# A sparse two-layer graph kernel: gather groups of 8 rows by 64 places, and the first head's relu on ScalarE

## The chip, the core and the metric

The kernel runs on one NeuronCore of a Trainium2 chip. Five engines work side by side, each on its own in-order list of instructions: TensorE (PE; its weight loads are shown as PEld), VectorE (DVE), ScalarE (ACT), GpSimd (POOL) and SyncE (SP). [...] The metric is device time in microseconds of one whole execution, as the median of several runs. A profiled execution gives a trace with every instruction; its span begins with the first and ends with the last of them.

## What is computed

Two graph layers over 3327 nodes with 128 features. The adjacency matrix is dense in memory but has only some 64 non-zero entries in a row. The first layer is an attention layer with four heads, and it holds nearly all of the work. Cut to what matters:

```python
h = jnp.maximum(_layernorm(x, axis=-1), 0.0)
def _gatv2_head(x, A_shape, w1, w2, a, Wlin):          # x is h here
    x1 = x @ w1
    x2 = x @ w2
    E = jax.nn.leaky_relu(x1[:, None, :] + x2[None, :, :], negative_slope=0.01)
    s = E @ a
    s = jnp.tanh(s / 8.0) * 8.0
    s = jnp.exp(s) * A_shape
    s = s / jnp.sum(s, axis=-1, keepdims=True)
    out = s @ x @ Wlin.T
    return jax.nn.leaky_relu(out, negative_slope=0.01)
x = x + jnp.concatenate([head(...) for 4 heads], axis=-1) @ w
# layer 1: relu(A_norm @ (h @ W.T + b)), A_norm from (adj + I) by row sums; x = x + that
```

Only pairs with a non-zero adjacency count, so the kernel makes scores for those pairs alone. With `leaky(e) = slope*e + (1-slope)*relu(e)`, a score is a linear part, which is made once for each node, and `(1-slope) * a . relu(x1 + x2)`, which has to be made for each pair and head.

## The kernel before

**Blocks, places and windows.** The 3328 padded rows are 26 blocks (`NB`) of 128 rows, and a block is done in two halves (`hb`) of 64 rows. While one block is scored, the next is prepared (`prep`, from line 353): its adjacency block is transposed in pieces on TensorE (line 365), copied by ScalarE (line 367) and stored by a DMA that ScalarE issues (line 370); VectorE finds the non-zero columns of each row with MAX8 and MATCH_REPLACE8 (lines 422 to 456). The result is a list `idx` with 64 places for each row; rows with more neighbours have the rest done in an overflow group.

**Gathers.** A table in HBM has one row for each node: its features, its four projections `x2` (one for each head), a linear score part, and columns of adjacency. A window `w` (four for a half block, `NW`) is a tile `g` of 8 slices; slice `t` is one indirect DMA (line 597) issued by GpSimd that brings 128 table rows onto the 128 partitions: 8 graph rows by 16 places. In the kernel before, the 8 slices of a window are the 64 rows of the half, and the four windows are the places 0 to 15, 16 to 31 and so on. Four buffers of `g` exist; a buffer is given back (`allow("g")`) behind the window's aggregation at line 702.

**Groups.** A half block is 9 groups: `m` = 0 to 7 are halves of windows (4 slices, so 512 pairs), `m` = 8 is the overflow. So there are 26 x 2 x 9 = 468 groups, and 26 x 2 x 8 = 416 of them are of the ordinary kind. `stage_z` does this for a pair of heads `hp` at a time:

- a PSUM tile `z` of two banks, one for each head of the pair (`ps_z`, two buffers);
- for each of the two heads four transposes on TensorE (line 624), which turn the projections of 4 slices, pairs on partitions, into features on partitions and 512 pairs along the row;
- one VectorE operation over both heads (line 640), `r = max(z, -x1)`, with `x1n = -x1` broadcast along the 16 places. As `max(z, -x1) = relu(z + x1) - x1`, the missing `x1` is a linear term, and `pex` (lines 563 to 570) adds it in the form `a . x1`.

`stage_r` (line 645) multiplies `r` by the vector `a` of each head (line 653, into the score tile `s`), one group later than `stage_z`. `finish` (line 657), once for each window, copies the scores to SBUF on ScalarE (line 662), transposes them back (line 671), adds the linear parts on VectorE (lines 674, 677), does tanh and exp on ScalarE (lines 682, 684), makes weights on VectorE (line 693) and aggregates the window on TensorE (line 702): eight matmuls, slice `t` into the column group `t % 4` (32 rows of PSUM each).

**What sets the order.** The order in each engine's list is written out by hand (`manual_schedule`). `slot()` (line 858) is called at six places of each group and gives out one step each of what is in progress: the `finish` of earlier windows, the tail of a half block (`close`), the preparation of the next block (`advance`), and the gathers. One `slot()` stands between the first and the second head's transposes of each pair (line 632). The framework puts in the semaphore waits, from which tile an instruction writes and which it reads.

**The queues.** GpSimd issues all gathers, 68 for a block. SyncE and ScalarE issue the other DMAs; a DMA that ScalarE issues stands in the same list as its arithmetic.

Of the kernel before, what the change touches and what calls it, by code (L numbers as in the profile page):

```python
# [9 lines left out]
F32 = mybir.dt.float32  # L10
AF = mybir.ActivationFunctionType
OP = mybir.AluOpType
# [3 lines left out]
P = 128  # L16
# [45 lines left out]
HALF = 64  # L62
OVT = 3
FOUND = 2
FEAT = 64
BODY = 648
# [165 lines left out]
def _sparse_layers(tc, nc, x, adj, w1, w2, a, wlin, w, gw, gb, gb_sb, gwT, x_sb, dinv, flag, ident, out):  # L232
# [24 lines left out]
    with ExitStack() as l0:  # L257
# [95 lines left out]
        def prep(b, k):  # L353
# [204 lines left out]
            for h in range(H):  # L558
                nc.tensor.matmul(pm[:, h * P:(h + 1) * P], w1_sb[:, h, :], hTb, start=True, stop=True)
            x1n = pb.tile([P, H, P], F32, name="x1n")  # L560
            nc.scalar.activation(x1n, pm[:, :H * P].rearrange("p (h i) -> p h i", h=H), AF.Copy, scale=-1.0)
            pmx = pb.tile([P, 16, H], F32, name="pmx")
            nc.vector.tensor_tensor(pmx, tmask[:, :, None].to_broadcast([P, 16, H]),
                                    p_all[:, b, None, :H].to_broadcast([P, 16, H]), OP.mult)
            yield
            yield
            pm = bank()
            nc.tensor.matmul(pm[:, :16 * H], modsel, pmx.rearrange("p t h -> p (t h)"), start=True, stop=True)
            pex = pb.tile([P, 16, H], F32, name="pex")
            nc.scalar.copy(pex, pm[:, :16 * H].rearrange("p (t h) -> p t h", h=H))  # L570
            k.x1b, k.x1n, k.pex = x1b, x1n, pex
            yield

        def rows_in():
            state["turn"] += 1
            return pgs[state["turn"] % 4].tile([P, WT, WIDE], F32, name="g")

        def gather(b, hb, w):

            k = blks[b]  # L580
            tab = tables[b % 2].rearrange("(r u) -> r u", u=1)
            if w == NW:
                if b + hb == 0:
                    state["over"] = pe_.tile([P, OVT, WIDE], F32, name="ge")
                    nc.vector.memset(state["over"][HALF:, FOUND:], 0.0)
                g, n, at = state["over"], FOUND, k.idxo[:, hb]
                rows = b * P + HALF * hb
                c0, n0 = (0, FEAT + COLS) if hb == 0 else (FEAT, BODY + FEAT)
                nc.sync.dma_start(g[:HALF, FOUND, :n0], tables[b % 2][:NP * ROW].rearrange("(r c) -> r c", c=ROW)[rows:rows + HALF, c0:c0 + n0])
            else:  # L590
                g, n, at = rows_in(), WT, k.idx[:, w, WT * hb:WT * hb + WT]

            def one(t):
                lo, hi = (0, FEAT + COLS) if hb == 0 else (0, BODY + FEAT)
                if w < NW:
                    lo, hi = (8 * t, hi) if hb == 0 else (0, BODY + 8 * t + 8)
                return nc.gpsimd.indirect_dma_start(out=g[:, t, lo:hi], out_offset=None, in_=tab,  # L597
                                                    in_offset=bass.IndirectOffsetOnAxis(ap=at[:, t:t + 1], axis=0))

            queue.extend((k, hb, w, partial(one, t)) for t in range(n))  # L600
            k.g[hb, w] = g
# [10 lines left out]
        def stage_z(k, hb, m, slot):  # L612
            n = 4 * P if m < 8 else FOUND * P
            arrived(k, hb, m // 2)
            g = k.g[hb, m // 2]
            out = []
            for hp in range(2):
                z = ps_z.tile([P, 2, BANK], F32, name="z")
                r = pr.tile([P, 2, BANK], F32, name=f"r{hp}")
                for i in range(2):  # L620
                    h = 2 * hp + i
                    c0 = k.f0[hb] + PROJ + h * D
                    for q in range(n // P):
                        nc.tensor.matmul(z[:, i, q * P:(q + 1) * P], g[:, m % 2 * 4 + q, c0:c0 + D], ident,  # L624
                                         is_transpose=True, start=(q == 0 or m < 8), stop=(m < 8), skip_group_check=True)
                    if m == 8:
                        nc.tensor.matmul(z[:, i, n:n + HALF], g[:HALF, FOUND, c0:c0 + D], ident[:HALF, :HALF],
                                         is_transpose=True, start=False, stop=False, skip_group_check=True)
                        nc.tensor.matmul(z[:, i, :n], k.x1b[:, h * D:(h + 1) * D], k.oi[:, hb * n:(hb + 1) * n],  # L629
                                         start=False, stop=True, skip_group_check=True)  # L630
                    if i == 0:
                        slot()
                slot()
                if m == 8:
                    nc.vector.tensor_tensor(r[:, :, n:n + HALF], z[:, :, n:n + HALF],  # L635
                                            k.x1n[:, 2 * hp:2 * hp + 2, HALF * hb:HALF * hb + HALF], OP.max)
                    nc.scalar.activation(r[:, :, :n], z[:, :, :n], AF.Relu)  # L637
                else:
                    r0 = HALF * hb + 32 * (m % 2)
                    nc.vector.tensor_tensor(r.rearrange("p h (i s) -> p h i s", s=16), z.rearrange("p h (i s) -> p h i s", s=16),  # L640
                                            k.x1n[:, 2 * hp:2 * hp + 2, r0:r0 + 32, None].to_broadcast([P, 2, 32, 16]), OP.max)
                out.append(r)
            return out

# [12 lines left out]
        def finish(k, hb, w):  # L657
# [1 line left out]
            f0 = k.f0[hb]  # L659
            nt, nk, nm = (WT, 4, 2) if w < NW else (OVT, OVT, 1)  # L660
            ssb = ph.tile([P, BANK], F32, name="ssb", bufs=1)
            nc.scalar.copy(ssb[:, :nk * P], s[:, :nk * P])  # L662
            if w < NW:
                wq = pb.tile([P, WT, 8], F32, name="wq")
                diag = bass.AP(g.tensor, g.offset + BODY * hb, [list(g.ap[0]), [WIDE + 8, 8], [1, 8]])
                nc.vector.tensor_tensor(wq, diag, qmask[:, None, :].to_broadcast([P, WT, 8]), OP.mult)
            yield
            yield
            pt = ps_tr.tile([P, 4, P], F32, name="tr")
            for q in range(nk):  # L670
# [3 lines left out]
            nc.vector.tensor_tensor(sc[:, :nt].rearrange("p (m k) h -> p m k h", m=nm),  # L674
                                    pt.rearrange("p k (h m) -> p m k h", m=32)[:, :nm, :nk],
                                    g[:, :, f0 + D:f0 + D + H].rearrange("p (m k) h -> p m k h", m=nm), OP.add)
            nc.vector.tensor_add(sc[:, :nt], sc[:, :nt], k.pex[:, 8 * hb:8 * hb + 8] if w < NW else  # L677
                                 k.ex[:, OVT * hb:OVT * hb + OVT, 42:42 + H])
            yield
            yield  # L680
            th = pb.tile([P, WT, H], F32, name="th")
# [9 lines left out]
            if w < NW:  # L691
                wt = pv.tile([P, WT, H, 8], F32, name="wt", bufs=2)
                nc.vector.tensor_tensor(wt, pe[:, :, :, None].to_broadcast([P, WT, H, 8]),  # L693
                                        wq[:, :, None, :].to_broadcast([P, WT, H, 8]), OP.mult)
                yield
                yield
                yield
                yield
                yield
                for t in range(WT):  # L700
                    u, cg = t // 4, t % 4
                    nc.tensor.matmul(ag[32 * cg:32 * cg + 32, u, :WORK], wt[:, t].rearrange("p h q -> p (h q)"),  # L702
                                     g[:, t, f0:f0 + WORK], start=(w == 0 and t < 4), stop=False, skip_group_check=True)
                allow("g")
                return
            am = pb.tile([P, OVT, HALF], F32, name="am", bufs=1)
# [649 lines left out]
```

## Time and profile before

| what | value |
|---|---|
| three runs: median, lowest, highest | 2523.51, 2521.55, 2527.58 us |
| the profiled execution: time, and its span | 2520.29 us, 2518.6 us |
| mean granted TensorE clock | 0.982 |
| VectorE busy, 400 to 2000 us, in stretches of 400 us | 352.23, 350.61, 351.86, 355.88 us |
| ScalarE busy, same stretches | 118.22, 110.82, 118.83, 111.55 us |
| DMA share, same stretches | 0.97, 0.97, 0.97, 0.98 |
| gathers, line 597: count, mean | 1664 and 104; 969 and 950 ns |
| first and last ordinary transpose of line 624 | 76.3 and 2409.4 us |

So some 76 us are preparation, some 2340 us are the 26 blocks (90 us each), and some 100 us at the end are the second layer.

A row of the table of groups reads: line, engine, operation, output<-input by tile name, shapes, count | busy us in all, mean ns of one | idle us of the engine just before them, and what ended that idle time. A row of the timeline reads: start in us, length in us, engine, line, operation, tiles, count of merged instructions, and in brackets the idle time before it. A row of the waits reads: who <- whom: us in total, times, longest. The mean of one matmul contains its way through the array, so matmuls that follow each other overlap and a row of several is shorter than their sum.

### The profile page before, as it was taken

The numbers are of one execution on the slowest core, as the hardware profiler recorded it, in microseconds if no ns is written. First come the engines' busy times: TensorE is split into PE (matmuls) and PEld (weight loads), VectorE is DVE, ScalarE is ACT, GpSimd is POOL, SyncE is SP. The second block draws the span as 40 slices with busy tenths as digits, with TensorE's granted clock in tenths as the row PEclk, the third lists the DMA queues.
The fourth block names the chain that finished last, engine by engine and source line by source line (L and its number), as shares of the span: only waits on it lengthen the run. The fifth ranks groups of instructions, "written<-read, shape, count | busy, mean of one in ns | idle before, by whom it ended". The sixth has DMA issues, their size and how long they took to land.

```text
span 2518.6 us, 52430 instructions
## 1 busy us (share of the span) xinstructions
PE 2283.0 (91%) x19410; PEld 1577.3 (63%) x19410; DVE 2091.0 (83%) x6478; ACT 686.3 (27%) x1703; POOL 1733.9 (69%) x1822
## 2 busy tenths in 40 slices
PE   6589999989999898999999999999999999999987
PEld 4456666666666666666666666666666666666643
DVE  7688988898898889889889888988988898895623
ACT  4122223223223222322322232232222223222110
POOL 3577777777777776777777777777777777777700
PEclk9799999999999999999999999999999999999999
DMA  9999999999999999999999999999999999999995
GB/s 307 377 359 325 344 340 312 339 358 319 323 356 334 316 341 336 298 333 357 331 317 349 347 311 333 354 321 319 344 339 316 338 348 310 328 325 351 347 275 153
DMA packets 417844, 826.94 MB, mean 328 GB/s; under 512 B 38435, under 2 KB 288815, under 8 KB 414255
## 3 DMA queue, kind: packets, MB, share of 16 engines
q0 software_dynamic: 141440, 619.41, 70.2%
q1 hardware_dynamic: 165343, 147.87, 18.5%
q10 hardware_dynamic: 110800, 56.25, 7.7%
q8 instruction: 156, 2.56, 0.4%
q14 instruction: 105, 0.86, 0.1%
HBM read 754.47 MB, written 113.22 MB: 345 GB/s over the span
## 4 chain that ended last, share of the span: by engine, by line
PE 36%; DVE 27%; DMA 19%; POOL 10%; issue 7%; ACT 1%; SPq 0%; DVEq 0%; ACTq 0%; POOLq 0%
DVE r L640 13%; DMA g<-table,idx 11%; PE z L624 11%; POOL g L597 9%; PE s L653 6%; PE z L629 3%; DVE cand L422 3%; DMA AT_d<-at 3%; PE tr L671 2%; PE ag L702 2%; DVE cand L456 2%; DVE lists L453 2%; DMA g<-AT_d 2%; DVE codes L410 2%; PE z L985 1%
## 5 line engine op out<-in xcount | busy, mean ns | idle before, releaser
L597 POOL DMA_INDIRECT g<-table,idx x1664 | 1611.9, 969 | 606.1 <-issue 416.3
L640 DVE TENSOR_TENSOR r<-z,x1n 128x1024 f32<-128x1024 f32 x832 | 1009.9, 1216 | 33.2 <-PE z L624 31.4
L624 PE MATMUL z<-ident,g 128*128 128x128 f32 x6656 | 918.6, 279 | 127.5 <-DVE r L640 110.6
L624 PEld LDWEIGHTS z<-ident,g 128*128 128x128 f32 x6656 | 746.4, 142 | 334.7 <-DVE r L640 222.2
L653 PE MATMUL s<-r,sel 128*2 128x512 f32 (+1 forms) x3744 | 473.6, 578 | 2.6 <-DVE s L650 1.9
L662 ACT COPY ssb<-s 128x512 f32<-128x512 f32 x260 | 146.9, 565 | 470.9 <-PE s L653 462.5
L422 DVE MAX8 cand<-codes 128x8 f32<-128x52 uint16 x1664 | 215.1, 204 | 0.0
L682 ACT ACTIVATE th<-sc 128x32 f32<-128x32 f32 x260 | 58.2, 224 | 459.8 <-DVE sc L677 422.3
L702 PEld LDWEIGHTS ag<-g,wt 128*32 128x32 f32 x3328 | 98.7, 110 | 120.3 <-issue 105.2
L671 PE MATMUL tr<-ident,ssb 128*128 128x128 f32 x988 | 157.0, 279 | 10.4 <-ACT ssb L662 9.0
L367 ACT COPY at<-tr 128x512 f32<-128x512 f32 (+1 forms) x175 | 97.1, 555 | 225.3 <-PE tr L365 194.1
L629 PE MATMUL z<-oi,x1b 128*128 128x256 f32 x416 | 145.4, 431 | 0.0
L453 DVE MAX8 lists<-cand 128x8 f32<-128x272 f32 (+1 forms) x338 | 133.2, 394 | 2.9
L702 PE MATMUL ag<-g,wt 128*32 128x133 f32 x3328 | 133.5, 278 | 1.5 <-DVE wt L693 1.5
L365 PE MATMUL tr<-ident,adjb 128*128 128x128 f32 x676 | 110.1, 287 | 25.2 <-DMA adjb<-in_adj_dram 17.7
L674 DVE TENSOR_TENSOR sc<-tr,g 128x32 f32<-128x32 f32 x208 | 38.5, 185 | 112.4 <-PE tr L671 112.4
L671 PEld LDWEIGHTS tr<-ident,ssb 128*128 128x128 f32 x988 | 111.0, 141 | 31.2 <-ACT ssb L662 23.4
L597 POOL DMA_INDIRECT ge<-table,idxo x104 | 98.8, 950 | 31.7 <-issue 14.0
L635 DVE TENSOR_TENSOR r<-z,x1n 128x128 f32<-128x128 f32 x104 | 29.9, 289 | 109.2 <-PE z L629 108.7
L637 ACT ACTIVATE r<-z 128x512 f32<-128x512 f32 x104 | 62.0, 597 | 212.5 <-DVE r L635 212.5
L456 DVE MATCH_REPLACE8 cand<-lists,cand 128x272 f32<-128x272 f32 (+1 forms) x312 | 118.1, 379 | 0.0
L410 DVE SCALAR_TENSOR_TENSOR codes<-adjb,code 128x832 uint16<-128x832 f32 x104 | 103.1, 1018 | 13.1 <-DMA adjb<-in_adj_dram 13.1
(201 smaller groups left out, 2446.0 us busy)
## 6 DMA issues: line engine op xcount, KB each, us to landing
adjb<-in_adj_dram SPq DMA_DIRECT2D x26, 1664.0 KB
table<-AT_d SPq DMA_DIRECT2D x26, 1664.0 KB
AT_d<-at ACTq DMA_DIRECT2D x150, 256.0 KB
g<-table,idx POOLq DMA_INDIRECT x1664
table<-img SPq DMA_DIRECT2D x12, 1296.0 KB
adjb<-AT_d SPq DMA_DIRECT2D x72, 128.0 KB
g<-AT_d SPq DMA_DIRECT2D x25, 256.0 KB
g<-AT_d ACTq DMA_DIRECT2D x25, 256.0 KB
```

The lines of the kernel that those rows point to most:

```text
L410: nc.vector.scalar_tensor_tensor(codes[:, i], adjb[:, c0:c0 + part], 0.0, code[:, c0:c0 + part], op0=OP.not_equal, op1=OP.mult, accum_out= ...
L422: nc.vector.max(cand[:, c, 8:].rearrange("p (r s) -> p r s", s=32)[:, :, sgm % 32], codes.rearrange("p a b -> p (a b)")[:, sgm % 32 * SEG: ...
L453: nc.vector.max(top, of)
L456: nc.vector.match_replace(out=of, in_to_replace=top, in_values=of, imm_value=0.0)
L597: return nc.gpsimd.indirect_dma_start(out=g[:, t, lo:hi], out_offset=None, in_=tab, in_offset=bass.IndirectOffsetOnAxis(ap=at[:, t:t + 1], ...
L624: nc.tensor.matmul(z[:, i, q * P:(q + 1) * P], g[:, m % 2 * 4 + q, c0:c0 + D], ident, is_transpose=True, start=(q == 0 or m < 8), stop=(m ...
L629: nc.tensor.matmul(z[:, i, :n], k.x1b[:, h * D:(h + 1) * D], k.oi[:, hb * n:(hb + 1) * n], start=False, stop=True, skip_group_check=True)
L640: nc.vector.tensor_tensor(r.rearrange("p h (i s) -> p h i s", s=16), z.rearrange("p h (i s) -> p h i s", s=16), k.x1n[:, 2 * hp:2 * hp + 2 ...
L653: nc.tensor.matmul(k.s[32 * h:32 * h + 2, :n], sel[:, h, 31 - at:33 - at], rs[h // 2][:, h % 2, :n], start=(at == 0), stop=(at == 1 or m = ...
L662: nc.scalar.copy(ssb[:, :nk * P], s[:, :nk * P])
L671: nc.tensor.transpose(pt[:, q, :], ssb[:, q * P:(q + 1) * P], ident)
L702: nc.tensor.matmul(ag[32 * cg:32 * cg + 32, u, :WORK], wt[:, t].rearrange("p h q -> p (h q)"), g[:, t, f0:f0 + WORK], start=(w == 0 and t ...
```

## The change

A window is now 16 rows with all 64 places: slice `t` of window `w` holds the 8 rows `8 * (2w + t // 4)` on, places `16 * (t % 4)` on. A group of 4 slices is 8 rows by 64 places, and the transposes write `z` in the order row, slice, place, in runs of 16 with a stride of 64. So all 64 columns of one row lie side by side, and share one `x1`. The first head's relu (`hp` = 0, `i` = 0) leaves VectorE: eight ScalarE operations, one for each row, read 64 columns of `z` with that row's `x1` as a pointer to a bias for each partition. They are given out straight behind the four transposes of that head, ahead of the `slot()`. VectorE's operation for the first pair covers the second head alone. The linear term of the first head changes from `a . x1` to `slope * a . x1` (the two VectorE operations for `pmx`). A plain copy `x1p` of the first head's `x1` is added for each block. The score copy `ssb` puts the columns back into the order slice, row, place. The aggregation writes for the two groups of the window into two column groups instead of four. The count and the bytes of the gathers are the same.

```diff
@@ prep
             nc.scalar.activation(x1n, pm[:, :H * P].rearrange("p (h i) -> p h i", h=H), AF.Copy, scale=-1.0)
+            x1p = pb.tile([P, P], F32, name="x1p")
+            nc.scalar.copy(x1p, pm[:, :P])
             pmx = pb.tile([P, 16, H], F32, name="pmx")
-            nc.vector.tensor_tensor(pmx, tmask[:, :, None].to_broadcast([P, 16, H]),
-                                    p_all[:, b, None, :H].to_broadcast([P, 16, H]), OP.mult)
+            for h0, h1, of in ((0, 1, H), (1, H, 0)):
+                nc.vector.tensor_tensor(pmx[:, :, h0:h1], tmask[:, :, None].to_broadcast([P, 16, h1 - h0]),
+                                        p_all[:, b, None, of + h0:of + h1].to_broadcast([P, 16, h1 - h0]), OP.mult)
@@ gather
+            t0 = WT * hb + 2 * w
             def one(t):
+                own = 8 * (2 * w + t // 4)
+                which = at[:, t % 4, t0 + t // 4:t0 + t // 4 + 1] if w < NW else at[:, t:t + 1]
...
@@ stage_z
+            r0 = HALF * hb + 8 * m
...
                     for q in range(n // P):
-                        nc.tensor.matmul(z[:, i, q * P:(q + 1) * P], g[:, m % 2 * 4 + q, c0:c0 + D], ident,
+                        to = z[:, i, q * P:(q + 1) * P] if m == 8 else z[:, i].rearrange("p (i q s) -> p q i s", q=4, s=16)[:, q]
+                        nc.tensor.matmul(to, g[:, m % 2 * 4 + q, c0:c0 + D], ident,
                                          is_transpose=True, start=(q == 0 or m < 8), stop=(m < 8), skip_group_check=True)
...
+                    if hp + i == 0 and m < 8:
+                        for e in range(8):
+                            nc.scalar.activation(r[:, 0, e * HALF:(e + 1) * HALF], z[:, 0, e * HALF:(e + 1) * HALF], AF.Relu,
+                                                 bias=k.x1p[:, r0 + e:r0 + e + 1], scale=1.0)
                     if i == 0:
                         slot()
...
-                    r0 = HALF * hb + 32 * (m % 2)
-                    nc.vector.tensor_tensor(r.rearrange("p h (i s) -> p h i s", s=16), z.rearrange("p h (i s) -> p h i s", s=16),
-                                            k.x1n[:, 2 * hp:2 * hp + 2, r0:r0 + 32, None].to_broadcast([P, 2, 32, 16]), OP.max)
+                    one = 1 - hp
+                    nc.vector.tensor_tensor(r[:, one:].rearrange("p h (i s) -> p h i s", s=HALF), z[:, one:].rearrange("p h (i s) -> p h i s", s=HALF),
+                                            k.x1n[:, 2 * hp + one:2 * hp + 2, r0:r0 + 8, None].to_broadcast([P, 2 - one, 8, HALF]), OP.max)
@@ finish
-            nc.scalar.copy(ssb[:, :nk * P], s[:, :nk * P])
+            if w < NW:
+                nc.scalar.copy(ssb.rearrange("p (q i s) -> p q i s", q=4, s=16), s.rearrange("p (i q s) -> p q i s", q=4, s=16))
+            else:
+                nc.scalar.copy(ssb[:, :nk * P], s[:, :nk * P])
...
-                for t in range(WT):
-                    u, cg = t // 4, t % 4
-                    nc.tensor.matmul(ag[32 * cg:32 * cg + 32, u, :WORK], wt[:, t].rearrange("p h q -> p (h q)"),
-                                     g[:, t, f0:f0 + WORK], start=(w == 0 and t < 4), stop=False, skip_group_check=True)
+                for q in range(4):
+                    for m in range(2):
+                        t, u, cg = 4 * m + q, (2 * w + m) // 4, (2 * w + m) % 4
+                        nc.tensor.matmul(ag[32 * cg:32 * cg + 32, u, :WORK], wt[:, t].rearrange("p h q -> p (h q)"),
+                                         g[:, t, f0:f0 + WORK], start=(w < 2 and q == 0), stop=False, skip_group_check=True)
```

More of the change, by code (lines that the diff above doesn't have):

```diff
@@ L570, in prep @@
             nc.scalar.copy(pex, pm[:, :16 * H].rearrange("p (t h) -> p t h", h=H))
-            k.x1b, k.x1n, k.pex = x1b, x1n, pex
+            k.x1b, k.x1n, k.x1p, k.pex = x1b, x1n, x1p, pex
             yield
@@ L590, in gather @@
             else:
-                g, n, at = rows_in(), WT, k.idx[:, w, WT * hb:WT * hb + WT]
+                g, n, at = rows_in(), WT, k.idx
+            t0 = WT * hb + 2 * w
             def one(t):
+                own = 8 * (2 * w + t // 4)
+                which = at[:, t % 4, t0 + t // 4:t0 + t // 4 + 1] if w < NW else at[:, t:t + 1]
                 lo, hi = (0, FEAT + COLS) if hb == 0 else (0, BODY + FEAT)
                 if w < NW:
-                    lo, hi = (8 * t, hi) if hb == 0 else (0, BODY + 8 * t + 8)
+                    lo, hi = (own, hi) if hb == 0 else (0, BODY + own + 8)
                 return nc.gpsimd.indirect_dma_start(out=g[:, t, lo:hi], out_offset=None, in_=tab,
-                                                    in_offset=bass.IndirectOffsetOnAxis(ap=at[:, t:t + 1], axis=0))
+                                                    in_offset=bass.IndirectOffsetOnAxis(ap=which, axis=0))
             queue.extend((k, hb, w, partial(one, t)) for t in range(n))
@@ L661, in finish @@
             ssb = ph.tile([P, BANK], F32, name="ssb", bufs=1)
-            nc.scalar.copy(ssb[:, :nk * P], s[:, :nk * P])
+            if w < NW:
+                nc.scalar.copy(ssb.rearrange("p (q i s) -> p q i s", q=4, s=16), s.rearrange("p (i q s) -> p q i s", q=4, s=16))
+            else:
+                nc.scalar.copy(ssb[:, :nk * P], s[:, :nk * P])
             if w < NW:
                 wq = pb.tile([P, WT, 8], F32, name="wq")
-                diag = bass.AP(g.tensor, g.offset + BODY * hb, [list(g.ap[0]), [WIDE + 8, 8], [1, 8]])
-                nc.vector.tensor_tensor(wq, diag, qmask[:, None, :].to_broadcast([P, WT, 8]), OP.mult)
+                diag = bass.AP(g.tensor, g.offset + BODY * hb + 16 * w, [list(g.ap[0]), [4 * WIDE + 8, 2], [WIDE, 4], [1, 8]])
+                nc.vector.tensor_tensor(wq.rearrange("p (m k) q -> p m k q", m=2), diag,
+                                        qmask[:, None, None, :].to_broadcast([P, 2, 4, 8]), OP.mult)
             yield
@@ L676, in finish @@
                                     g[:, :, f0 + D:f0 + D + H].rearrange("p (m k) h -> p m k h", m=nm), OP.add)
-            nc.vector.tensor_add(sc[:, :nt], sc[:, :nt], k.pex[:, 8 * hb:8 * hb + 8] if w < NW else
-                                 k.ex[:, OVT * hb:OVT * hb + OVT, 42:42 + H])
+            if w < NW:
+                t0 = WT * hb + 2 * w
+                sc_v = sc.rearrange("p (m k) h -> p m k h", m=2)
+                nc.vector.tensor_tensor(sc_v, sc_v, k.pex[:, t0:t0 + 2, None, :].to_broadcast([P, 2, 4, H]), OP.add)
+            else:
+                nc.vector.tensor_add(sc[:, :nt], sc[:, :nt], k.ex[:, OVT * hb:OVT * hb + OVT, 42:42 + H])
             yield
```

## The prediction

> **What bounds the kernel now.** I read the page's shares of the engines and its chain of waits first, then the groups by line, the list of waits, and the timeline of single groups.
>
> ```profile
> PE 2283.0 (91%) x19410; PEld 1577.3 (63%) x19410; DVE 2091.0 (83%) x6478; ACT 686.3 (27%) x1703; POOL 1733.9 (69%) x1822
> PE 36%; DVE 27%; DMA 19%; POOL 10%; issue 7%; ACT 1%; SPq 0%; DVEq 0%; ACTq 0%; POOLq 0%
> L640 DVE TENSOR_TENSOR r<-z,x1n 128x1024 f32<-128x1024 f32 x832 | 1009.9, 1216 | 33.2 <-PE z L624 31.4
> L637 ACT ACTIVATE r<-z 128x512 f32<-128x512 f32 x104 | 62.0, 597 | 212.5 <-DVE r L635 212.5
> ```
>
> Several engines are close to full at once: TensorE at 91%, VectorE at 83% with half of it in line 640, and the gathers, whose 1768 issues follow each other 1.25 us apart (starts at 1111.43, 1112.68, 1113.94 in GpSimd's timeline). ScalarE alone has room. The row of line 637 is read for something else: in the overflow group ScalarE writes columns 0 to 255 of `r` and VectorE (line 635) columns 256 to 319, from the same `z`; they touch no common element, yet ScalarE waits for VectorE, 212.5 us over 104 times. Waits are set by the tile, not by the columns.
>
> ```profile
> PEld z L624 <- DVE r L640: 248.8, 240, 3.0
> PE z L624 <- DVE r L640: 112.1, 144, 2.6
> POOL g L597 <- PE ag L702: 68.2, 42, 3.6
> ```
>
> This is all that VectorE's relief can give back: TensorE's wait for line 640, at least the 112.1 us in which the array stood empty, at most the 248.8 of the weight loads and 26.5 more for the `ge` form of line 624. Beyond it GpSimd comes next; its own wait for the window buffers is 68.2 us.
>
> ```profile
> 1246.26 1.04 PE L653 MATMUL s<-r,sel 128*2 128x512 f32 x8
> 1247.12 0.64 PE L702 MATMUL ag<-g,wt 128*32 128x133 f32 x16
> 1247.69 0.66 PE L624 MATMUL z<-ident,g 128*128 128x128 f32 x4
> 1248.18 0.60 PE L671 MATMUL tr<-ident,ssb 128*128 128x128 f32 x4
> 1248.62 1.52 PE L624 MATMUL z<-ident,g 128*128 128x128 f32 x12
> 1250.07 1.04 PE L653 MATMUL s<-r,sel 128*2 128x512 f32 x8
> ```
>
> One ordinary group when nothing holds TensorE up: 3.81 us, and the four transposes of the first head are followed, behind the slot's work, by the other twelve without a gap.
>
> **The change part by part.** *The new wait.* In the changed program as it is built, the fifth transpose of each first pair, the second head's first, carries a wait on ScalarE's semaphore, and so does VectorE's operation of that pair; both are for the eighth relu of the same tile. It is the rule that line 637 shows: `z` is one tile, ScalarE reads its first bank, and what TensorE writes into it afterwards is ordered behind that. TensorE's list is in order, so all behind the fifth transpose stands still: the other eleven of the group, the previous group's scores, the aggregation, and whoever waits for those. The price comes from these rows:
>
> ```profile
> L737 ACT ACTIVATE agn<-ag,rec 128x128 f32<-128x128 f32 x104 | 32.6, 364 | 58.3 <-DVE rec L732 32.0 <-DMA g<-AT_d 20.8 <-DVE part L385 4.1
> 1146.09 0.63 ACT L737 ACTIVATE agn<-ag,rec 128x128 f32<-128x128 f32 x2 [0.44 <-DVE rec L732]
> 6.87 1.28 ACT L1055 ACTIVATE cen<-x_sb,neg 128x128 f32<-128x128 f32 x4 [0.67 <-DVE neg L1046]
> 1187.68 0.19 ACT L490 COPY lists<-rowid 128x1 f32<-128x1 f32 x1
> 1187.78 0.20 ACT L491 COPY lists<-p_all 128x4 f32<-128x4 f32 x1
> 1255.60 1.04 PE L653 MATMUL s<-r,sel 128*2 128x512 f32 x8
> 1256.70 0.59 ACT L662 COPY ssb<-s 128x512 f32<-128x512 f32 x1
> 1260.14 0.48 ACT L662 COPY ssb<-s 128x384 f32<-128x384 f32 x1 [1.05 <-PE s L653]
> 1260.67 0.31 PEld L671 LDWEIGHTS tr<-ident,ssb 128*128 128x128 f32 x3 [0.25 <-ACT ssb L662]
> ```
>
> The nearest operation is line 737: from PSUM, with one pointer operand, 128 columns. One takes 364 ns, two in a row 0.63 us, so they follow each other 0.63 - 0.364 = 0.266 us apart. The copies of line 662 give the price of a column, (586 - 479) / 128 = 0.84 ns, so 64 columns fewer are 0.054 us less: 0.212 us apart, 0.31 us for the last. Eight take 7 x 0.212 + 0.31 = 1.80 us. The bounds: from SBUF (line 1055, four in 1.28 us, mean 389 ns) they are 0.297 us apart, 0.243 at 64 columns, which gives 7 x 0.243 + 0.335 = 2.04 us; the small copies of lines 490 and 491, without a pointer, start 0.10 us apart, 0.15 with 64 columns, which gives 1.36 us. I take 1.80, as line 737 reads PSUM and has the pointer. [...]
>
> Around them: four transposes end 0.60 us after they start, while the fifth could have started after 0.44 (the twelve: (1.52 - 0.66) / 8 = 0.108 us apart); TensorE's end to ScalarE's start is 0.06 us (1256.64 to 1256.70), ScalarE's end to TensorE's start 0.05 (1260.62 to 1260.67). So the gap is 0.60 - 0.44 + 0.06 + 1.80 + 0.05 = 2.07 us. It is partly filled: the slot between the two heads gives TensorE work of its own. In the built program that is, over the 416 first pairs, 981 score transposes and 286 adjacency transposes (0.108 us each, 137 us) and 306 overflow aggregations, 96 matmuls of line 470 and 12 of 512 columns, each two instructions (0.11 us, about a transpose's pace at about its length; 0.10, as eight of line 470 take 0.80 in the chain; 0.43, as two of line 553 take 1.02 with a mean of 0.59: 97 us): 234 us, or 0.56 for a pair. The net gap is 1.51 us, and 416 of them are **+628 us**. If that cover were gone, it would be 861.
>
> *ScalarE's list.* A relu also waits for what stands ahead of it there: copies `at` of 0.59 us with a DMA issue of 0.37 us behind (seven for a block), line 443 (2.98 us, once for a block, but right behind a relu and so beside 4 us of TensorE work), the tail's activations that wait for VectorE. The busy time per group outside the relus is 686 / 468 = 1.47 us; in a group of some 6.5 us, of which the relus take 1.8, ScalarE is in one of these operations 1.47 / 4.7 = 0.31 of the time, and some 0.6 us of it and its followers are left: 0.2 us, 416 times **+83 us**. Bounds: nothing, if they always finish within the other 4.7 us, and 0.5 us (208 us), if one `at` with its issue is ahead each second time.
>
> *The aggregation.* The 16 instructions of line 702 take 0.64 us with a mean of 278 ns, four at a time in the four column groups: 0.28 + 3 steps of 0.12. With two column groups it is 0.28 + 7 x 0.12, or 0.49 us more on TensorE, 208 times: **+102 us**. The bounds are 0, if the instructions of one column group overlap, and 102.
>
> *VectorE's relief.* Line 640 for the first pair falls to 512 columns; line 952 has that shape at 689 ns, so 416 x (1216 - 689) = 219 us less busy time. Its worth is TensorE's wait above, 112 to 275 us; I take **-200**, as the matmul row leaves out what the array still drains, some 0.2 us each of 384 times. With 6.4 us for a group VectorE's remaining 4.0 us no longer press.
>
> *Hidden.* `x1p` (0.27 us on ScalarE, 26 times), the split `pmx` (0.2 us on VectorE, 26 times) and the reordered copy `ssb` (same columns) lie beside TensorE's work: zero, 12 us if that cover were gone. Gathers: the same count and bytes; with longer groups GpSimd's 85 us for a block (68 x 1.25) and the DMA queues have room. The strided writes into PSUM have no row; I take nothing, since the count of columns is the same; the upper bound is the spread between the rows of four, 0.60 and 0.66 us, 0.015 us for each of 6656 transposes or 100 us; the lower bound is zero, as the writes can't become denser than side by side.
>
> *Sum.* 2520.3 (the profiled execution, 1.7 us above its span and 3.2 below the median) + 628 + 83 + 102 - 200 = **3133 us**, say 3130. That is 23 us more for each of the 26 blocks, 113 instead of 90. Both ends: 2520 + 628 - 183 + 0 + 0 - 275 = 2690 and 2520 + 628 + 100 + 208 + 102 + 100 - 112 = 3546. That all go one way is unlikely.
>
> The clock: from 84 to 88 us, with no matmul at all, the granted clock was 0.51, and from 1180 to 1182, with 0.95 us of work, 1.00. A gap of 2 us in each 6 is like the second. [...]
>
> **The rivals.** (a) *VectorE was the bound and ScalarE runs beside it*: TensorE isn't held, since the two banks are apart. Speaking for it: VectorE is full from 1126 to 1166 us and 27% of the chain. Against it: line 637, and the wait in the built program. TensorE then gains its 112 to 200 us, pays 102, and GpSimd's buffers allow 68 at most: 2450 to 2500, faster. It decides if the fifth transpose starts less than 0.3 us behind the slot's work. Chance 0.02. (b) *Not held, but the aggregation counts*: 2520 + 102 with half the ScalarE delay, 2600 to 2700. Chance 0.03; no change at all would need these to cancel, 0.01. (c) *ScalarE's list is the longer wait*: relus behind `at` copies and behind activations that themselves wait for VectorE, 0.5 us or more a pair instead of 0.2: 3133 + 416 x 0.3 = 3260 at least, up to 3500. For it: 0.96 us for each `at` with its issue. Against: ScalarE would be busy 1440 of 3130 us only. Chance 0.12. (d) *Cheaper relus and full relief*: 1.36 us for eight and 275 given back, 3133 - 183 - 75 = 2875, or 2750 to 3000 around it. For it: the pace of the small copies. Against: they have no pointer. Chance 0.10.
>
> **How the numbers follow.** The forecast, held by the new wait, 2940 to 3320, has 0.72; its time is the sum, 3130. The range is that same stretch: of (c) and (d) about a third falls into it too, 0.07, and 2 in 10 are left out on both sides together. A difference of 0.2%, 5 us, is about what a measurement of this kernel can tell from none. Faster is (a) 0.02, the same 0.01, slower the rest, 0.97.
>
> **What would show it.** The second head's transposes should have ScalarE's relu as releaser of their idle time, some 1.5 us a pair and over 600 us in all; the chain should pass from VectorE to ScalarE; eight relus should take 1.8 us; the new line 702 some 1.1 us for 16 instructions; VectorE's share should fall to about 60%, GpSimd's to 55%. The forecast is wrong if TensorE's idle time before these transposes is below 200 us, or if the granted clock falls under 0.9.

## The result, and the profile after

| | median | lowest to highest | profiled execution | its span |
|---|---|---|---|---|
| before | 2524.17 us (4 runs) | 2521.55 to 2527.58 | 2520.29 us | 2518.6 us |
| after | 3057.26 us (4 runs) | 3051.57 to 3066.46 | 3051.57 us | 3049.9 us |

The ratio is 1.211, with an interval from 1.208 to 1.215: the change costs 533 us, some 20 us for each of the 26 blocks.

The shares of the engines, and the chain of waits by engine, after:

```profile
PE 2438.8 (80%) x19410; PEld 1678.0 (55%) x19410; DVE 1920.8 (63%) x6504; ACT 1386.9 (45%) x5057; POOL 1756.7 (58%) x1822
PE 68%; ACT 23%; DVE 4%; DMA 3%; issue 2%; ACTq 0%; SPq 0%; DVEq 0%
```

TensorE has as many instructions as before and yet fell from 91% to 80% of a longer span: 3049.9 - 2438.8 = 611 us idle, 2518.6 - 2283.0 = 236 before. VectorE has gone from the chain (27% to 4%), as have GpSimd (10% to none) and most of the DMA (19% to 3%); ScalarE stands there with 23%, at only 45% busy. An engine that is busy for less than half of the span now takes part in setting the end, by where its work lies.

The groups by line say before which instruction TensorE stands idle:

```profile
L633 PE MATMUL z<-ident,g 128*128 128x128 f32 x6656 | 948.9, 283 | 538.3 <-ACT r L642 533.3
L653 DVE TENSOR_TENSOR r<-z,x1n 128x512 f32<-128x512 f32 x832 | 792.4, 952 | 546.3 <-PE z L633 539.0
L642 ACT ACTIVATE r<-z,x1p 128x64 f32<-128x64 f32 x3328 | 727.6, 329 | 391.4 <-PE z L633 370.9
L724 PE MATMUL ag<-g,wt 128*32 128x133 f32 x3328 | 226.9, 279 | 0.0
```

Line 633 (624 before) waits 533.3 us for line 642, the relus on ScalarE. Line 653 (640 before) waits 539.0 us for line 633, since its second head comes late; the relus in their turn wait 370.9 us for line 633. TensorE and ScalarE so wait for each other in turn, and VectorE waits for TensorE: none of the three is full. The list of waits has the same wait as the weight loads meet it, and what became of GpSimd:

```profile
PEld z L633 <- ACT r L642: 622.5, 365, 8.3
PE z L633 <- ACT r L642: 533.3, 365, 7.5
POOL g L604 <- PE z L633: 423.1, 155, 8.2
```

The gathers were as good as paced by GpSimd itself before (68.2 us of wait for window buffers); now the profile puts 423.1 us of their wait down to the transposes, which read the windows and come late. One group in the timeline:

```profile
1504.52 1.04 PE L666 MATMUL s<-r,sel 128*2 128x512 f32 x8
1505.39 1.08 PE L724 MATMUL ag<-g,wt 128*32 128x133 f32 x16
1506.40 0.66 PE L633 MATMUL z<-ident,g 128*128 128x128 f32 x4
...
1507.09 1.75 ACT L642 ACTIVATE r<-z,x1p 128x64 f32<-128x64 f32 x8 [3.74 <-PE z L633]
...
1508.89 1.53 PE L633 MATMUL z<-ident,g 128*128 128x128 f32 x12 [1.84 <-ACT r L642]
1509.66 0.69 DVE L653 TENSOR_TENSOR r<-z,x1n 128x512 f32<-128x512 f32 x1 [0.76 <-PE z L633]
1510.36 1.04 PE L666 MATMUL s<-r,sel 128*2 128x512 f32 x8
```

Four transposes, ScalarE's eight relus 0.03 us behind them, and 0.05 us after their end the other twelve; in between the array is empty for 1.84 us. From one group's scores to the next it is 5.84 us, against 3.81 in the group shown of the kernel before.

To place the whole loss, I took from the trace the start of each of the 16 transposes of the 416 ordinary groups, and summed how much later than the usual 0.109 us it follows the start of the instruction ahead of it:

```
extra time in front of   1st    5th    9th   13th transpose   sum (us)
before                 144.2    4.4   78.4    4.8              232
after                   80.1  597.0    2.5    6.0              686
own_tiles               87.2    5.2   35.0    4.3              132
behind                 285.0    6.8   10.3    6.3              308
one_relu                79.9  195.4   16.0    4.6              296
```

The lower rows are of the experiments below. The first transpose needs a free tile of the first pair, the ninth one of the second: VectorE's wait for these lies in the two columns, whose sum falls from 222.6 to 82.6 us. What is left of it in the row `after` is hardly a wait: the array is empty for only 2.1 us in front of these first transposes, and the 80.1 us are mostly the slower pace of the instruction ahead (107 of them follow a score matmul of 512 columns, at 0.41 us over the usual in the median, 44 us in all). The fifth is the second head's first, and there 597.0 us have come in.

### The profile page after: what moved, and what is told of

The parts are those of the page before. It is cut to its first block, busy times and chain, and to the rows that moved or that the text cites. A ratio compares the mean times of both kernels' runs of the same rounds, so it can differ in the third digit from the quotient of the medians.

```text
span 3049.9 us, 56288 instructions
## 1 busy us (share of the span) xinstructions
PE 2438.8 (80%) x19410; PEld 1678.0 (55%) x19410; DVE 1920.8 (63%) x6504; ACT 1386.9 (45%) x5057; POOL 1756.7 (58%) x1822
## 4 chain that ended last, share of the span: by engine, by line
PE 68%; ACT 23%; DVE 4%; DMA 3%; issue 2%; ACTq 0%; SPq 0%; DVEq 0%
PE z L633 26%; ACT r L642 19%; PE s L666 13%; PE ag L724 6%; PE z L638 4%; PE ag L743 3%; ACT adjb L443 2%; PE tr L379 2%; DVE r L653 1%; PE tr L365 1%; PE z L636 1%; DMA g<-AT_d 1%; PE z L1007 1%; DVE codes L410 1%; PE tr L688 1%
## 5 line engine op out<-in xcount | busy, mean ns | idle before, releaser
L604 POOL DMA_INDIRECT g<-table,idx x1664 | 1634.4, 982 | 1088.4 <-PE z L633 423.1
L633 PE MATMUL z<-ident,g 128*128 128x128 f32 x6656 | 948.9, 283 | 538.3 <-ACT r L642 533.3
L633 PEld LDWEIGHTS z<-ident,g 128*128 128x128 f32 x6656 | 745.0, 143 | 794.8 <-ACT r L642 622.5
L653 DVE TENSOR_TENSOR r<-z,x1n 128x512 f32<-128x512 f32 x832 | 792.4, 952 | 546.3 <-PE z L633 539.0
L642 ACT ACTIVATE r<-z,x1p 128x64 f32<-128x64 f32 x3328 | 727.6, 329 | 391.4 <-PE z L633 370.9
L666 PE MATMUL s<-r,sel 128*2 128x512 f32 (+1 forms) x3744 | 481.5, 587 | 2.6 <-DVE s L663 1.9
L676 ACT COPY ssb<-s 128x512 f32<-128x512 f32 x208 | 122.0, 586 | 310.6 <-PE s L666 306.2
L724 PEld LDWEIGHTS ag<-g,wt 128*32 128x32 f32 x3328 | 189.6, 111 | 128.5 <-issue 102.4
L724 PE MATMUL ag<-g,wt 128*32 128x133 f32 x3328 | 226.9, 279 | 0.0
```

Of the source, the lines that this page charges most:

```text
L633: nc.tensor.matmul(to, g[:, m % 2 * 4 + q, c0:c0 + D], ident, is_transpose=True, start=(q == 0 or m < 8), stop=(m < 8), skip_group_check=True)
L642: nc.scalar.activation(r[:, 0, e * HALF:(e + 1) * HALF], z[:, 0, e * HALF:(e + 1) * HALF], AF.Relu, bias=k.x1p[:, r0 + e:r0 + e + 1], scal ...
L653: nc.vector.tensor_tensor(r[:, one:].rearrange("p h (i s) -> p h i s", s=HALF), z[:, one:].rearrange("p h (i s) -> p h i s", s=HALF), k.x1 ...
L666: nc.tensor.matmul(k.s[32 * h:32 * h + 2, :n], sel[:, h, 31 - at:33 - at], rs[h // 2][:, h % 2, :n], start=(at == 0), stop=(at == 1 or m = ...
```

## The experiments

The theory: TensorE is held because both heads of the pair share one tile `z`, and its writes for the second head are ordered behind ScalarE's reads of the first. The rivals: it is ScalarE's added work, wherever it stands; it is the place in the list; it is the aggregation in two column groups.

**Tiles of its own for each head (own_tiles).** The relus stay where they are. For the first pair each head gets a tile `z` of one bank and a tile `r`; the overflow group's first pair is split by head in the same way.

```diff
-                z = ps_z.tile([P, 2, BANK], F32, name="z")
-                r = pr.tile([P, 2, BANK], F32, name=f"r{hp}")
+                if hp == 0:
+                    zs = [ps_z.tile([P, BANK], F32, name=f"z{i}") for i in range(2)]
+                    rr = [pr.tile([P, BANK], F32, name=f"r0{i}") for i in range(2)]
...
-                            nc.scalar.activation(r[:, 0, e * HALF:(e + 1) * HALF], z[:, 0, e * HALF:(e + 1) * HALF], AF.Relu,
+                            nc.scalar.activation(rr[0][:, e * HALF:(e + 1) * HALF], zs[0][:, e * HALF:(e + 1) * HALF], AF.Relu,
```

> The changed kernel, but the first pair has a z tile of one bank and an r tile for each head, so that the second head's transposes and VectorE's operation share no tile with the relus, which stay where they are. Theory (the tile's wait holds TensorE): the 597 us that TensorE stood in front of the fifth transpose go, 3052 - 597 = 2455; the aggregation's 93 us stay in, VectorE stays relieved, and GpSimd, which waited 68 us for buffers before, allows no less than about 2445. So 2450 to 2570 us, and the releaser ACT r vanishes from the waits of z. Rival (the eight operations fill ScalarE's list, or the new layout costs it): 2900 us or more, with the delay moved to other ScalarE waits.

Measured: 2557.76 us, ratio 1.013 (1.011 to 1.014); the kernel before took 2524.59 beside it. The shares of the engines, two rows of its groups and one of its waits:

```profile
PE 2390.4 (93%) x19410; PEld 1668.6 (65%) x19410; DVE 1900.0 (74%) x6556; ACT 1387.9 (54%) x5109; POOL 1753.8 (68%) x1822
```

```profile
L637 PE MATMUL z<-ident,g 128*128 128x128 f32 x6656 | 915.1, 279 | 34.2 <-DVE r L665 17.6
L646 ACT ACTIVATE r<-z,x1p 128x64 f32<-128x64 f32 x3328 | 728.1, 330 | 352.2 <-PE z L637 329.2
```

```profile
PEld z L637 <- ACT r L646: 54.9, 67, 5.0
```

A group with no hold in its timeline:

```profile
1304.24 1.08 PE L736 MATMUL ag<-g,wt 128*32 128x133 f32 x16
1305.25 0.66 PE L637 MATMUL z<-ident,g 128*128 128x128 f32 x4
1305.74 0.60 PE L700 MATMUL tr<-ident,ssb 128*128 128x128 f32 x4
1306.18 1.47 PE L637 MATMUL z<-ident,g 128*128 128x128 f32 x12
```

ScalarE does the same 3328 relus in the same 728 us, and TensorE's wait before line 637 is 34.2 us, 17.6 of it for VectorE: the twelve follow the four and the slot's work without a gap, and the extra time in front of the fifth transpose is 5.2 us. The releaser that was to vanish from the waits of `z` keeps 54.9 us of the weight loads' idle time, where it had 622.5 in the change. So 500 of the 533 us (3057.26 - 2557.76) are the shared tile, and not ScalarE's work. The experiment splits `r` together with `z`; but what TensorE writes, and so waits with, is `z` alone. The split needs no more room: two tiles of one bank and one of two make four banks, as the two tiles of two banks did.

**The relus behind the second head (behind).** Shared tile as in the change, but the eight relus are given out after VectorE's operation of the pair.

```diff
-                    if hp + i == 0 and m < 8:
-                        for e in range(8):
-                            nc.scalar.activation(r[:, 0, e * HALF:(e + 1) * HALF], ...
...
                                             k.x1n[:, 2 * hp + one:2 * hp + 2, r0:r0 + 8, None].to_broadcast([P, 2 - one, 8, HALF]), OP.max)
+                    if hp == 0:
+                        for e in range(8):
+                            nc.scalar.activation(r[:, 0, e * HALF:(e + 1) * HALF], ...
```

> The changed kernel, but the eight relus are given out behind the second head's transposes and behind VectorE's operation of that pair. The tiles are shared as before. Theory: the fifth transpose isn't held; the tile comes free 0.69 + 1.75 us behind the second head, and TensorE wants it again after its second pair (0.87), the scores (0.97) and the slots' work (about 1): mostly hidden, 2480 to 2650 us, with some wait for ACT r in front of the first transpose instead. Rival (ScalarE's list or the layout): as the changed kernel, 2950 us or more.

Measured: 2770.82 us, ratio 1.100 (1.097 to 1.102), far above what was expected. Its groups and its waits:

```profile
L633 PE MATMUL z<-ident,g 128*128 128x128 f32 x6656 | 931.1, 284 | 200.2 <-ACT r L653 191.1
L653 ACT ACTIVATE r<-z,x1p 128x64 f32<-128x64 f32 x3328 | 725.9, 330 | 904.0 <-DVE r L649 884.0
```

```profile
PEld z L633 <- ACT r L653: 335.9, 182, 4.4
POOL g L604 <- PE ag L724: 344.1, 148, 7.3
DVE wt L714 <- ACT pe L705: 119.7, 99, 6.3
```

The hold in front of the fifth transpose is gone (6.8 us), but two others have come. VectorE now uses the pair's tiles first, and ScalarE's list stands 884.0 us behind it; whatever follows the relus there stands too, and VectorE's line 714 waits 119.7 us for the exp of line 705. And `z` comes free only when both engines have been through it, one after the other: 285.0 us in front of the first transpose, against 80.1 in the change. The expectation had the two engines' time in a row on one tile (0.69 + 1.75 us) and took it for mostly hidden; what it had not was that ScalarE's whole list then stands behind VectorE. The clock has a part too: the granted mean is 0.960, against 0.974 in the change (the last section has the windows).

**One relu instead of eight (one_relu).** It leaves out `x1` of the first head: one ScalarE operation over 512 columns, without a bias.

```diff
-                        for e in range(8):
-                            nc.scalar.activation(r[:, 0, e * HALF:(e + 1) * HALF], z[:, 0, e * HALF:(e + 1) * HALF], AF.Relu,
-                                                 bias=k.x1p[:, r0 + e:r0 + e + 1], scale=1.0)
+                        nc.scalar.activation(r[:, 0], z[:, 0], AF.Relu)
```

> The changed kernel with one ScalarE operation of 512 columns without a bias in place of the eight of 64 (it leaves out x1 from the first head's relu). The wait stays. Theory: 0.60 instead of 1.75 us stand in the gap, 2.08 becomes 0.93, of which the slot's work covers a larger share; 597 us fall to between 120 and 240, so 2570 to 2700 us. Rival (layout, aggregation): unchanged near 3050. If the count of ScalarE operations rather than their length counted, the gap would fall to nearly nothing: below 2520.

Measured: 2655.95 us, ratio 1.053 (1.051 to 1.056), within what was expected.

```profile
L633 PE MATMUL z<-ident,g 128*128 128x128 f32 x6656 | 937.3, 280 | 159.9 <-ACT r L641 140.7
L641 ACT ACTIVATE r<-z 128x512 f32<-128x512 f32 x416 | 248.0, 596 | 387.7 <-PE z L633 367.5
```

ScalarE's stay in the tile falls from 1.749 us (mean of the eights in the trace) to 0.596, by 1.15 us, and the extra time in front of the fifth transpose from 597.0 to 195.4, by 0.97 us for each of the 416. The hold follows the length of ScalarE's work, and the tile is held even when that work is short.

**The aggregation's order (before_two_groups).** The kernel before, with the eight slices of line 702 so ordered that only two column groups come at a time.

```diff
-                for t in range(WT):
+                for t in (0, 1, 4, 5, 2, 3, 6, 7):
```

> The kernel before with the slices of a window aggregated in the order 0, 1, 4, 5, 2, 3, 6, 7, so that at any time two of the four column groups are fed, as in the changed kernel. Theory: 16 instructions take 1.1 instead of 0.64 us, 93 us more of TensorE work; where TensorE already waits for VectorE it hides, so 20 to 100 us more, 2540 to 2620. Rival (the aggregation is hidden or the array finds the four groups anyway): within 10 us of before.

Measured: 2524.09 us, ratio 1.0005 (0.9994 to 1.0017), and

```profile
L702 PE MATMUL ag<-g,wt 128*32 128x133 f32 x3328 | 138.1, 281 | 1.1 <-DVE wt L693 1.1
```

That is 138.1 us busy, against 133.5 in the kernel before and 226.9 after. The order alone does not make the condition: each column group still has two slices of the window (four instructions of the sixteen), where the change gives each of two groups four slices. The run therefore says nothing on the price of the aggregation in the change.

**Four column groups again, and half a block (own_four, after_four, before_two, half).** These were to show what the remaining 33 us of own_tiles are. The kernel own_four is own_tiles, and after_four the changed kernel, with the slices written to four column groups as before; before_two is the kernel before with two. All three add slices under wrong rows and so leave out the right places of the sums; half keeps the change with tiles of its own for the first half of each block, and the second half stays on VectorE in the old order.

```diff
-                for q in range(4):
-                    for m in range(2):
-                        t, u, cg = 4 * m + q, (2 * w + m) // 4, (2 * w + m) % 4
+                for m in range(2):
+                    for q in range(4):
+                        t, u, cg = 4 * m + q, m, q
```

> own_tiles with line 702's aggregation fed to four column groups in the order of the kernel before, though the slices hold other rows now (it sums the wrong slices, so the output isn't the reference's; the instructions are as many and as long). Theory (without the tile's wait TensorE is the bound, and its busy time grew by the aggregation's 93 us): 2558 - 93 = 2465, or somewhat more where GpSimd becomes the bound, 2450 to 2500 us. Rival (ScalarE's waits or the split overflow operations cost own_tiles its time): 2530 to 2560.

> The changed kernel with the same four column groups (it sums the wrong slices). Theory (TensorE's list is one chain here, so its work adds up): 3052 - 93 = 2960, 2940 to 2980 us. Rival (the aggregation lies in time that is lost anyway): above 3020.

> The kernel before with each window aggregated into two column groups only, 2 * (w % 2) + t % 2 (the sums are of the wrong slices); the order alone didn't do it. Theory: 16 instructions take 1.1 us, 93 us more TensorE work; TensorE idles 9% of the span here and waits for VectorE, so some of it hides: 2550 to 2610 us. Rival: it hides wholly, within 10 us of before.

> own_tiles for the first half of each block alone, in which VectorE is full with the lists of the next block; the second half has the windows, the relu on VectorE and the aggregation of the kernel before. Theory: half of the aggregation's 93 us goes, and most of VectorE's relief stays: 2490 to 2530 us, so at or a little below the kernel before. Rival (TensorE waits for VectorE in the second half as much as it gains): 2540 to 2580 us.

> own_tiles for the first half of each block alone, in which VectorE is full with the lists of the next block; the second half has the windows, the relu on VectorE and the aggregation of the kernel before. Theory: half of the aggregation's 93 us goes, and most of VectorE's relief stays: 2490 to 2530 us, so at or a little below the kernel before. Rival (TensorE waits for VectorE in the second half as much as it gains): 2540 to 2580 us.

> own_tiles with line 702's aggregation fed to four column groups (it sums the wrong slices; the instructions are as many and as long), to be read on a chip where the kernel before takes its 2524 us. Theory (without the tile's wait TensorE is the bound, and its busy time grew by the aggregation's 93 us): 2558 - 93 = 2465, or somewhat more where GpSimd becomes the bound, 2450 to 2500 us. Rival (ScalarE's waits or the split overflow operations cost own_tiles its time): 2530 to 2560.

> Tiles of its own for each head as in the run own_tiles, and the aggregation's eight slices written to four column groups as in the kernel before (leaves out the right places of the sums: slices are added under wrong rows). On a chip where the kernel before takes some 2524 us. Theory: what own_tiles still loses to the kernel before (1.0127, some 32 us) is the aggregation in two column groups, 93 us more of TensorE, less VectorE's relief. Then 2450 to 2500 us, ratio 0.970 to 0.990, and line 738's matmuls busy some 130 to 145 us instead of 227. Rival: the aggregation has cover and the loss is ScalarE's work and the second list of waits: 2530 to 2560 us, ratio 1.002 to 1.015, with the aggregation's busy time falling all the same.

> The same kernel as in own_four_3 once more, in the hope of a chip on which the kernel before takes some 2524 us (leaves out the right places of the sums). Theory, there: what own_tiles still loses to the kernel before, some 32 us, is the aggregation in two column groups, so 2450 to 2500 us, ratio 0.970 to 0.990. Rival, there: the aggregation has cover, and the loss is the second list of waits: 2530 to 2560 us, ratio 1.002 to 1.015. On a chip where the kernel before takes some 3380 us: ratio 1.060 to 1.066 as in the runs before it, and the question stays open.

| run | median, kernel before beside it | ratio and interval |
|---|---|---|
| own_four | 3604.92, 3385.96 us | 1.063 (1.059 to 1.066) |
| after_four | 4008.68, 3385.96 us | 1.185 (1.181 to 1.189) |
| before_two | 3452.46, 3385.96 us | 1.020 (1.017 to 1.024) |
| half, which leaves out part of the second half's sums | 3541.04, 3385.96 us | 1.047 (1.044 to 1.050) |
| half_2, with those sums | 3538.25, 3389.51 us | 1.040 (1.036 to 1.045) |
| own_four_2, own_four with the first window's start flag on four slices instead of eight | 3605.68, 3389.51 us | 1.063 (1.060 to 1.066) |
| own_four_3, the kernel of own_four_2 | 3594.77, 3377.47 us | 1.064 (1.060 to 1.068) |
| own_four_4, the same | 3508.58, 3315.93 us | 1.057 (1.054 to 1.061) |

None of these answers the question for the runs above. They ran on four other chips, and there the unchanged kernel before took 3316 to 3390 us, a third more than the 2524 us of all the runs above, so that neither their times nor their ratios can be set beside those. From half_2's waits and timeline:

```profile
PEld z L637 <- issue: 268.5, 365, 10.9
PEld ag L749 <- issue: 239.0, 514, 2.0
```

```profile
1514.91 0.08 PEld L687 LDWEIGHTS s<-r,sel 128*2 128x2 f32 x1 [0.64 <-issue]
1516.34 0.08 PEld L687 LDWEIGHTS s<-r,sel 128*2 128x2 f32 x1 [1.34 <-issue]
```

Here TensorE waits for nothing that the profile shows: 1.34 us in the second of these lines, and up to 10.9 us in the list. In own_tiles the longest such wait in front of the aggregation's weight loads was 0.7 us, and their sum 83.0. Within a single chip three comparisons hold. After_four against own_four, which differ in the shared tiles alone, is 4008.68 - 3604.92 = 404 us: the main finding stands on a second chip as well. Before_two against the kernel before is 3452.46 - 3385.96 = 66 us, the price of two column groups in that kernel there. And own_four, with its four column groups, is still 219 us slower than the kernel before: on that chip the rest of the change costs time too, without the two column groups. What the aggregation costs in own_tiles, and whether a version such as half beats the kernel before on a chip like that of the first runs, stays open.

## Why the prediction held, step by step

**The direction and the mechanism.** The forecast was 3130 us in a range of 2940 to 3320; the time is 3057. The releaser named for the second head's transposes is the one in the trace, at 622.5 us of the weight loads' idle time and 533.3 us of an empty array (over 600 was foretold, without saying which of the two), and own_tiles shows that it is the shared tile: with it taken away, 500 us go. Row 637 of the kernel before, ScalarE waiting for VectorE although they touch different columns, was the right row to read.

**The net gap, +628.** Measured 597.0, with all delay of ScalarE's list in it. Eight relus take 1.749 us, where 1.80 was the estimate, so the rows of line 737 were near. From the fourth transpose's start to the fifth's it is 2.18 us in the mean, 2.07 above the usual 0.109, which is just the estimate; 597.0 / 416 = 1.44 us of it stand in front of the fifth itself, so the slot's work covers 0.64 us, where 0.56 was reckoned from the built program.

**ScalarE's list, +83.** This is the term that was mis-sized. The relus start 0.038 us behind the fourth transpose in the median, and over 416 groups the starts come to 34.9 us; what exceeds the median, 34.9 - 416 x 0.038, is 19 us. I had let ScalarE's other work fall evenly over the time. The likely reason why it doesn't, argued and not tested: the relus stand ahead of the slot in its list, so that what the slot gives it comes just behind them, and TensorE's hold gives it time to end: in the group shown ScalarE had been idle for 3.74 us when the relus came. Rival (c), ScalarE's list as the longer wait, falls by the same starts, 19 us in all, and by the relus' own wait of 370.9 us for TensorE.

**The aggregation, +102.** Line 724 is busy 226.9 us, line 702 was 133.5: 93 us, and sixteen take 1.08 us instead of 0.64. That all of it lies on the path is argued from TensorE's place in the chain (68%); the runs that were to measure it are those of the other chips. In own_tiles the accounts can be set out by busy time alone: TensorE is 2390.4 - 2283.0 = 107 us busier than before, and idle 172.7 instead of 235.6, or 63 less; 107 - 63 is the 44 us by which its span is longer than before's.

**VectorE's relief, -200.** By what remains it is 2520.3 + 597.0 + 93 - 3051.6 = 159 us, within the bounds of 112 to 275, if all of the 93 us lie on the path. Of it 140 are seen directly, in front of the first and ninth transposes (222.6 to 82.6). I had added 0.2 us for each wait as what the array drains, an estimate that no run shows, and by these numbers it was too much.

**The sum** missed the profiled execution by 3133 - 3051.6 = 81 us, and these are: 114 too much for the wait with the list (628 + 83 - 597) and 9 too much for the aggregation, less 41 too much of relief. So the errors went in part against each other, which was luck. Leaving out the list's delay but for its 19 us would have given 3069.

**What was put at nothing.** The strided writes into PSUM cost nothing: the mean of a transpose in own_tiles is 279 ns as before, with TensorE 93% busy. The gathers found room: the DMA share, 0.97 before, is 0.83 to 0.86 between 400 and 2000 us.

**The clock.** The granted clock is 0.974 in the mean, against 0.982 before, and 0.99 in each stretch of 400 us from 400 to 2000 us; a mean under 0.9, by which the forecast would have been wrong, did not come. But I had read too little out of a single row when I took a hold of 2 us for harmless; the last section shows how near halved windows lie.

**The other rivals.** (a), ScalarE running beside, is what the change would have been with separate tiles, and even own_tiles lies at 2557.76, above the 2450 to 2500 given for it: TensorE there idles 63 us less than before, where 112 to 200 were given, and is 107 us busier, where 102 were. (b) and (d) need the wait to be absent, or eight relus at 1.36 us; neither is in the trace.

## What to carry to other kernels

In this kernel a second engine that took over part of a tile's work held up the engine that writes the other part, as long as both were one tile: before moving work, look in the trace for two engines that use different columns of one tile and see whether one waits for the other. The price of such a hold was here the new operation's length and the hand-overs around it (1.75 + 0.32 = 2.07 us), less whatever the in-order engine was given to do between the write and the held instruction, times the number of groups; give each half a tile of its own and the hold goes, as 500 of the 533 us did here. Moving the operation behind the other engine's instead (behind) took away 286 of the 533 us and moved the rest, to the release of the tile and to all that stands behind the operation on its own engine.

## What was not expected of the hardware

Here the matmuls of 32 columns of weights in four column groups run beside each other even when only two groups come at a time: 138.1 us busy in the reordered kernel before, against 133.5 in order, and 226.9 where each window has only two groups for all sixteen. In the median of the 208 windows of the kernel before, four instructions start within 0.02 us, and the next four 0.11 us later; in the changed kernel two start within 0.01 us, and the next two 0.11 us later. So here it is how many instructions each group has that counts; their order moves the end of the sixteen by some 0.02 us (0.66 us against 0.64).

In the traces of the kernel before and of the change the granted clock goes between 1.00 and 0.50, in stretches of 3.41 us or a multiple of it (6.83, 10.24 us); nine of the ten halved windows of the change from 400 to 2000 us follow one that holds a wait of 1.84 to 1.89 us for the relus. Four windows of the changed kernel between such bounds, TensorE alone (columns: the window, its length, the busy time and count of matmuls, the granted clock, the DMA share, GB/s):

```profile
1473.52:1476.93 3.41, 2.05 (x20) 1.00 0.65 157
1476.94:1480.35 3.41, 1.52 (x15) 1.00 1.03 294
1480.36:1483.76 3.40, 3.40 (x18) 0.50 0.95 366
1483.77:1487.18 3.41, 2.14 (x28) 1.00 0.98 402
```

The second window holds one wait for the relus of 1.89 us and nothing else that is idle, and the window after it runs at half the clock, 0.50, with TensorE busy for all of its 3.40 us. Of the 469 windows from 400 to 2000 us the changed kernel has 10 that are halved, each behind one with 1.39 to 1.58 us of work; the kernel before has 8, behind 0.54 to 1.56 us; every window with more than 1.58 us of work in these two was followed by a full one, some with 1.53 to 1.58 too. So the window ahead of a halved one was not idle in these two traces: TensorE worked in it for 0.54 to 1.58 of 3.41 us. No sharp bound shows: in own_tiles one halved window stands behind 1.74 us of work. The holds cost the clock next to nothing here (10 x 3.41 us at half speed against 8). The run behind has more of them: counted in the same way, 29 halved windows of 469. They come in 18 groups, each behind a window with 1.10 to 1.53 us of work, and 11 of the groups last two windows.

On the four other chips the same unchanged kernel took 3316 to 3390 us instead of 2524. In the profiled runs there (all of kernels with an edit) TensorE's instructions come late where nothing seen in the profile holds them, in half_2 by up to 10.9 us, the mean granted clock is 0.84 to 0.90, and in own_four_2 10% of the chain of waits is put down to "another core or an unknown queue", which the profiles of the kernel before and of the change don't have. What makes them so was not found.
